# A graph layer on one core: the prologue put in a hand-set order, with x in pieces of 5 to 15 nodes a partition, the dst and edge-weight rows asked for later, and the check tables spread over the first passes

## The chip, the cores and the metric

The kernel runs on one core of one Trainium2 chip. The metric is the device time of an execution in microseconds (us). Three runs of the kernel before gave 2122.5, 2125.32 and 2127.98 us; the median is 2125.32.

Five engines work beside each other, each through its own list of instructions in order: TensorE (PE, matrix products), VectorE (DVE), ScalarE (ACT), GpSimd (POOL) and SyncE (SP). They wait for each other through semaphores. A DMA can be asked for from SP's, ACT's or POOL's list; an instruction that asks for a DMA may itself have to wait, and then everything behind it in that engine's list waits too.

## The reference

One layer of a graph network over N = 12500 nodes of D = 128 features and M = 200000 edges, sorted by target node `dst`:

```python
h = jnp.maximum(_layernorm(x, axis=-1), 0.0)
Qv = h @ W_Q.T;  Ku = h @ W_K.T
score = jnp.einsum('md,md->m', Qv[dst], Ku[src]) / np.sqrt(128) * jnp.exp(-edge_weight)
# of each target's edges the 16 with the highest scores are kept; softmax over them gives alpha
agg = segment_sum(alpha[:, None] * (h[src] @ W_msg.T), dst)
out = x + relu(h @ W_self.T + agg)
```

So every edge needs the normalised row h[src] of its source node, and these rows lie anywhere in the table.

## The kernel before

**Main loop (from L383).** Edges are cut into 112 windows of 14 chunks of 128 edges. For each chunk POOL issues one gather (L399, an indirect DMA): it fetches the 128 rows h[src] from the table `h_tab` in device memory into the tile `hs` (7 buffers of one window each). That makes 1563 gathers. A pass of the loop works on several windows at once: in pass i it lets go the gathers of window i+2 (`let_go`, L405: DVE copies the indices to `ix`, POOL gathers), computes scores of window i (L500), picks the 16 best of window i-2, forms weights of window i-3 and sums (L580, L590), and stores window i-5. The order of all this is written out by hand (`manual_schedule`), pass by pass. The gathers of windows 0 and 1 take their indices straight from `idx_all`, before the first pass. SP's list holds the loads of node rows (`load_nodes`, L422), of dst broadcast over the partitions (`load_dst`, L432) and the stores.

**Prologue (L103 to L356).** Before the loop, the kernel

- loads x in ten pieces of 10 nodes per partition on 125 partitions, each as two DMAs on SP (112 and 13 partitions, L235);
- normalises each piece: DVE computes mean and variance per node (L241, L242), ACT the square root (L245), DVE the reciprocal and the bias (L246, L248); DVE then applies them to two nodes of ten and ACT to eight (L252, L255); two SP stores write the piece to `h_tab` (L261);
- loads src, dst and edge weights as rows (121 partitions), four weight matrices and the window bounds `b_i`, all asked for on ACT;
- turns src, positions, decays and dst from rows to columns through PE (`to_columns`, L206): `idx_all`, `pos_all`, `dec_all`, `dst_all`;
- computes from dst the position of each edge among its target's edges (is_equal and a scan, L320, L321), window tables (`bb`, `nb`, `dlw`), and tables that check the assumptions of the fast path (`own`, `bad`, L322 to L356). If a check fails, a general path after the loop (`tc.If` on `any_i`) computes the layer instead; with these inputs it does not run.

The prologue's order on each engine is not written by hand: the framework's scheduler sets it. The memory of the pieces (`prep`) and of the late tables (`late`) is given back before the loop's tiles are made. Gathers read all of `h_tab`, so the first gather waits for the last store to it.

The transfers of SP and ACT take eight completion semaphores in turn; one that takes a semaphore again waits first for the transfer that had it last.

Of the kernel before, what the change touches and what calls it, by code (L numbers as in the profile page):

```python
# [20 lines left out]
P = 128  # L21
# [53 lines left out]
def gnn_layer(  # L75
# [58 lines left out]
    make_identity(nc, ident)  # L134
    ones = const.tile([P, 1], F32, name="ones")
    nc.vector.memset(ones, 1.0)
    onerow = const.tile([1, P], F32, name="onerow")
    nc.vector.memset(onerow, 1.0)
    zrow = const.tile([1, WW], BF16, name="zrow")
    nc.vector.memset(zrow, 0.0)  # L140
# [4 lines left out]
    for i in range(2):  # L145
        nc.gpsimd.memset(alz[i], 0.0)
        nc.gpsimd.memset(sl1[i][:, :, KM:], 1.0)
    slots = const.tile([P, KM], F32, name="slots")
    nc.gpsimd.iota(slots, pattern=[[1, KM]], base=0, channel_multiplier=0,
                   allow_small_or_imprecise_dtypes=True)  # L150
    nvec = const.tile([P, 1], F32, name="nvec")
    nc.gpsimd.iota(nvec, pattern=[[0, 1]], base=0, channel_multiplier=1,
                   allow_small_or_imprecise_dtypes=True)
# [15 lines left out]

    rows_pool = ctx.enter_context(tc.tile_pool(name="rows", bufs=1))  # L170


    with tc.tile_pool(name="edges", bufs=1) as ep:
        src_r = ep.tile([RR, RW], I32, name="src_r")
        dst_r = ep.tile([RR, HALO + RW], I32, name="dst_r")
        ew_r = ep.tile([RR, RW], F32, name="ew_r")

# [5 lines left out]

        nc.gpsimd.memset(src_r, 0)
        load_rows(src_r, src)
        nc.gpsimd.iota(dst_r, pattern=[[1, HALO + RW]], base=1 << 21, channel_multiplier=0)
        nc.gpsimd.memset(dst_r[0:1, 0:HALO], -1)
        nc.scalar.dma_start(dst_r[0:1, HALO:], dst[0:RW].rearrange("(p c) -> p c", p=1))
        if RF > 1:
            nc.scalar.dma_start(dst_r[1:RF, :], bass.AP(dst.tensor, dst.offset + RW - HALO,  # L190
                                                        [[RW, RF - 1], [1, HALO + RW]]))
        if REM:
            nc.scalar.dma_start(dst_r[RF:RF + 1, 0:HALO + REM],
                                dst[RF * RW - HALO:M].rearrange("(p c) -> p c", p=1))
        b_i = ep.tile([1, G], I32, name="b_i")
        nc.scalar.dma_start(b_i[:, 1:G], bass.AP(dst.tensor, dst.offset + EG - 1, [[EG, 1], [EG, G - 1]]))
        nc.gpsimd.memset(ew_r, 0.0)
        load_rows(ew_r, ew)

        wq_sb = ep.tile([P, P], F32, name="wq_sb")  # L200
        wk_sb = ep.tile([P, P], F32, name="wk_sb")
        ws_sb = ep.tile([P, P], F32, name="ws_sb")
        wm_sb = ep.tile([P, P], F32, name="wm_sb")
        for t, w in ((wq_sb, w_q), (wk_sb, w_k), (ws_sb, w_self), (wm_sb, w_msg)):
            nc.scalar.dma_start(t, w)
# [12 lines left out]
        src_f = src_r.bitcast(F32)  # L218
        nc.vector.tensor_copy(src_f, src_r)
        to_columns(src_f, 0, lambda at, p: nc.vector.tensor_copy(at(idx_all), p))  # L220

        HP = largest_divisor(N, P)
        HT = N // HP
        HG = largest_divisor(HT, 10)
        cuts = [(0, HP - HP % 16), (HP - HP % 16, HP)]
        by_part = lambda a: a[0:N, :].rearrange("(p t) d -> p t d", t=HT)
        with tc.tile_pool(name="prep", bufs=2) as prep:
            xs = []  # L230
            for g0 in range(0, HT, HG):
                xg = prep.tile([HP, HG, D], F32, bufs=HT // HG, name="xg")
                for a, b in cuts:
                    if a < b:
                        nc.sync.dma_start(xg[a:b], by_part(x)[a:b, g0:g0 + HG, :])  # L235
                xs.append(xg)
            for i, xg in enumerate(xs):
                mv = prep.tile([HP, HG, 2], F32, name="mv")
                for t in range(HG):
                    st = prep.tile([HP, 6], F32, bufs=4, name="st")  # L240
                    nc.vector.bn_stats(st, xg[:, t, :])  # L241
                    nc.vector.bn_aggr(mv[:, t, :], st)  # L242
                rs = prep.tile([HP, HG], F32, name="rs")
                nc.vector.tensor_scalar(rs, mv[:, :, 1], EPS, None, op0=OP.add)
                nc.scalar.sqrt(rs, rs)  # L245
                nc.vector.reciprocal(rs, rs)  # L246
                nm = prep.tile([HP, HG], F32, name="nmr")
                nc.vector.scalar_tensor_tensor(nm, mv[:, :, 0], -1.0, rs, op0=OP.mult, op1=OP.mult)  # L248
                few = HG // 5
                for t in range(HG):  # L250
                    if t < few:
                        nc.vector.tensor_scalar(xg[:, t, :], xg[:, t, :], rs[:, t:t + 1], nm[:, t:t + 1],  # L252
                                                op0=OP.mult, op1=OP.add)
                    else:
                        nc.scalar.activation(xg[:, t, :], xg[:, t, :], AF.Relu, bias=nm[:, t:t + 1],  # L255
                                             scale=rs[:, t:t + 1])
                if few:
                    nc.vector.tensor_scalar(xg[:, 0:few, :], xg[:, 0:few, :], 0.0, None, op0=OP.max)
                for a, b in cuts:
                    if a < b:  # L260
                        nc.sync.dma_start(by_part(h_tab)[a:b, i * HG:(i + 1) * HG, :], xg[a:b])  # L261
        zpad = ep.tile([P, D], F32, name="zpad")
        nc.gpsimd.memset(zpad, 0.0)
        nc.sync.dma_start(h_tab[N:N + P, :], zpad)
        nc.sync.dma_start(x_end[XT:XT + P, :], zpad)
        nc.sync.dma_start(x_end[0:XT, :], x[N - XT:N, :])

        pw = bank("s", 1)
        nc.tensor.matmul(pw[:, 0:P], lhsT=wq_sb, rhs=wk_sb, start=True, stop=True)
        nc.scalar.mul(a_qk, pw[:, 0:P], 1.0 / math.sqrt(D))  # L270
        pw = bank("s", 1)
        nc.tensor.transpose(pw[:, 0:P], ws_sb, ident)
        nc.tensor.transpose(pw[:, P:2 * P], wm_sb, ident)
        nc.scalar.copy(wselfT, pw[:, 0:P])
        nc.scalar.copy(wmsgT, pw[:, P:2 * P])


        row = ep.tile([1, 4, G + 1], F32, name="row")
        first, used, count = row[:, 0, 0:G], row[:, 1, 0:G], row[:, 2, 0:G]
        bad = ep.tile([P, 4], F32, name="bad")  # L280
        nc.vector.memset(bad, 0.0)
        nc.vector.memset(row, 0.0)
        nc.vector.tensor_scalar(row[:, 0, 1:G], b_i[:, 1:G], 1.0, None, op0=OP.add)
        nc.vector.memset(row[:, 0, G:G + 1], float(N))
        nc.vector.tensor_sub(count, row[:, 0, 1:G + 1], first)
        nc.vector.tensor_copy(used, first)
# [4 lines left out]
        nc.vector.memset(row_i[:, 1, :], 0)  # L291
        nc.vector.tensor_copy(row_i[:, 1, G - TAIL:G], row[:, 3, 0:TAIL])

# [6 lines left out]
        pb = bank("s", 1)  # L300
        nc.tensor.matmul(pb[:, 0:G], lhsT=onerow, rhs=used, start=True, stop=True)
        nc.tensor.matmul(pb[:, G:2 * G], lhsT=onerow, rhs=count, start=True, stop=True)
        bb = ep.tile([P, 2, G], F32, name="bb")
        nc.vector.tensor_copy(bb, pb[:, 0:2 * G].rearrange("p (a g) -> p a g", a=2))
        nc.vector.tensor_scalar(nb, bb[:, 0, :], nvec, -1.0, op0=OP.add, op1=OP.mult)
# [8 lines left out]
        RL = HALO + RW  # L314
        dst_f = dst_r.bitcast(F32)
        nc.vector.tensor_copy(dst_f, dst_r)
        h0 = ep.tile([RR, RL], F32, name="h0")
        h1 = ep.tile([RR, RL], F32, name="h1")
        nc.vector.memset(h0[:, 0:1], 0.0)
        nc.vector.tensor_tensor(h0[:, 1:RL], dst_f[:, 1:RL], dst_f[:, 0:RL - 1], op=OP.is_equal)  # L320
        nc.vector.tensor_tensor_scan(h1, h0, h0, 0.0, op0=OP.mult, op1=OP.add)  # L321
        nc.vector.tensor_reduce(bad[0:RR, 0:1], h1[:, HALO:RL], axis=AX.X, op=OP.max)  # L322
        nc.vector.tensor_scalar(bad[0:RR, 0:1], bad[0:RR, 0:1], float(KM), None, op0=OP.is_ge)
        nc.vector.scalar_tensor_tensor(h0[:, HALO:RL], dst_f[:, HALO - 1:RL - 1], 0.0, dst_f[:, HALO:RL],
                                       op0=OP.add, op1=OP.is_gt, accum_out=bad[0:RR, 1:2])
        nc.vector.memset(pos_all[:, RR * CPR:CW], 0.0)
        nc.vector.memset(dec_all[:, RR * CPR:CW], 0.0)
        to_columns(h1, HALO, lambda at, p: nc.vector.tensor_copy(at(pos_all), p))
        to_columns(ew_r, 0, lambda at, p: nc.scalar.activation(at(dec_all), p, AF.Exp, scale=-1.0))
        dst_all = ep.tile([P, CW], F32, name="dst_all")  # L330
        nc.vector.memset(dst_all[:, RR * CPR:CW], float(1 << 21))
        to_columns(dst_f, HALO, lambda at, p: nc.scalar.copy(at(dst_all), p))

        with tc.tile_pool(name="late", bufs=1) as lp:

            w0 = lp.tile([P, NJ], F32, name="w0")
            for j in range(NJ):
                nc.vector.memset(w0[:, j:j + 1], float(lead(j)))
            own = lp.tile([P, G, NJ], F32, name="own")
# [518 lines left out]
```

## Time and profile before

| what | us |
|---|---|
| median of three runs | 2125.32 |
| profiled execution: its own time / span in the trace | 2125.5 / 2123.7 |
| busy: PE, DVE, ACT, POOL | 1312.0, 1488.2, 626.7, 1544.1 |
| one gather: median, mean | 0.944, 0.975 |
| start of the first gather, start of the last | 79.86, 2084.51 |
| first copy of indices (`ix`) by DVE for a gather | 100.09 |
| issue of the first x load, of the last store of a piece | 0.78, 75.32 |

The span is counted from the first instruction of the program to the last; the profiled execution's own time is 1.8 us longer. A row of the timeline gives the start, the length, the engine and line, what is written and read, the shapes, how many instructions were merged, and in brackets the idle time of that engine before it and what ended it. "issue" there means that nothing that the profile shows was waited for. SPq and ACTq rows are DMA requests in an engine's list. In a view by stretches the last two numbers are the mean busy share of the core's 16 DMA engines and the GB/s they moved.

### The profile page before, as it was taken

To read this page: it belongs to the slowest core of one execution; us is meant where nothing else is said; L and a number is where in the kernel's file an instruction comes from. 1 tells how busy PE (TensorE), PEld (TensorE's weight loads), DVE (VectorE), ACT (ScalarE), POOL (GpSimd) and SP (SyncE) were. 2 spreads that over 40 slices of the span, in tenths; PEclk is the share of its full clock that TensorE was granted. 3 is DMA by queue.
4 is the path that set the end of the run, shared out by engine and by line. 5 is a ranking of instruction groups with operands and counts; after the bars stand their busy time and mean duration, and the time that the engine had idled before them with its cause. 6 is when DMAs were issued, how large, how long until landed. Compare 5 with 4: busy or idle time off the path is not lost. (4 is left out here: it accounts for less than half of the span.)

```text
span 2123.7 us, 43559 instructions
## 1 busy us (share of the span) xinstructions
PE 1312.0 (62%) x14574; PEld 1210.1 (57%) x14575; DVE 1488.2 (70%) x7474; ACT 626.7 (30%) x1225; POOL 1544.1 (73%) x1585
## 2 busy tenths in 40 slices
PE   1166666666666666666666666666666666666665
PEld 1155566555555655555555656565666666565654
DVE  7667677777776777767777767677777776777764
ACT  3442222222222222222222222222222222222220
POOL 1477777777777777777777777777777777777773
PEclk9977877877777877877777777777777787877787
DMA  8453343333343343333333334334433343333420
GB/s 220 146 162 116 119 120 119 120 119 119 120 119 119 116 122 115 115 112 119 118 119 119 119 119 120 119 119 120 120 119 120 119 120 120 119 119 119 120 67 24
DMA packets 118805, 253.18 MB, mean 119 GB/s; under 512 B 33030, under 2 KB 76297, under 8 KB 118558
## 3 DMA queue, kind: packets, MB, share of 16 engines
q1 hardware_dynamic: 67336, 144.92, 19.7%
q0 software_dynamic: 50144, 102.74, 19.1%
q10 hardware_dynamic: 1094, 2.69, 0.5%
q8 instruction: 115, 1.88, 0.4%
q14 instruction: 116, 0.95, 0.1%
HBM read 236.40 MB, written 14.40 MB: 118 GB/s over the span
## 5 line engine op out<-in xcount | busy, mean ns | idle before, releaser
L399 POOL DMA_INDIRECT hs<-h_tab,ix x1535 | 1495.9, 975 | 467.8 <-issue 335.9
L500 DVE SCALAR_TENSOR_TENSOR prod<-hs,dec_all,q 128x128 f32<-128x128 f32 x1674 | 516.9, 345 | 334.3 <-DMA hs<-h_tab,ix 319.1
L490 PE MATMUL q<-q,to_e 128*128 128x128 bf16 x5022 | 464.2, 254 | 33.1 <-DVE prod L500 32.3
L598 PE MATMUL s<-ident,agn 128*128 128x128 f32 x112 | 49.3, 440 | 662.2 <-DVE kept L579 661.7
L490 PEld LDWEIGHTS <-to_e 128*128 128x128 bf16 x5022 | 410.1, 116 | 56.0 <-issue 39.8
L590 PE MATMUL a<-hs,alz 128*128 128x128 f32 x3348 | 425.8, 281 | 0.8 <-DVE alz L580 0.8
L598 PEld LDWEIGHTS s<-ident,agn 128*128 128x128 f32 x112 | 20.2, 180 | 678.4 <-issue 676.7
L590 PEld LDWEIGHTS a<-hs,alz 128*128 128x128 f32 x3348 | 404.4, 197 | 1.2 <-DVE alz L580 1.1
L515 PE MATMUL e<-ow,sl 128*41 128x40 f32 x3348 | 251.3, 265 | 8.4 <-DVE sl L508 8.4
L515 PEld LDWEIGHTS e<-ow,sl 128*41 128x41 f32 x3348 | 235.7, 184 | 23.6 <-DVE sl L508 9.2
L466 ACT ACTIVATE far<-dstb,nb 128x1920 bf16<-128x1920 int32 x112 | 212.9, 1901 | 5.1 <-DMA dstb<-in_dst_dram 5.1
L471 ACT ACTIVATE to_e<-far 128x1920 bf16<-128x1920 bf16 x112 | 201.2, 1796 | 0.1
L602 ACT COPY aggT<-s 128x128 f32<-128x128 f32 x112 | 29.8, 266 | 507.8 <-PE s L598 507.8
L529 DVE TENSOR_SCALAR ell<-slots,e 128x40 f32<-128x40 f32 x112 | 28.3, 253 | 205.3 <-PE e L515 192.6
L546 ACT ACTIVATE e<-v,km 128x16 f32<-128x16 f32 x112 | 34.4, 308 | 363.5 <-DVE km L538 363.5
L500 DVE DVE_READ_ACCUMULATOR prod<-hs,dec_all,q 128x1 f32 x1674 | 139.1, 83 | 0.2
L414 DVE COPY ix<-idx_all 128x2 int32<-128x2 int32 (+1 forms) x768 | 132.7, 173 | 0.0
L575 ACT ACTIVATE up<-up 128x15 f32<-128x15 f32 x112 | 24.1, 215 | 336.5 <-DVE up L567 336.4
L595 ACT ACTIVATE agn<-a,rden 128x128 f32<-128x128 f32 x112 | 41.2, 368 | 209.8 <-PE a L590 209.8
L508 DVE TENSOR_TENSOR sl<-po,s 128x600 f32<-128x600 f32 x112 | 87.5, 781 | 3.9
L580 DVE TENSOR_TENSOR alz<-ow,kept 128x600 f32<-128x600 f32 x112 | 87.5, 781 | 3.8
L399 POOL DMA_INDIRECT hs<-h_tab,idx_all x28 | 33.7, 1203 | 77.6 <-DMA x_end<-zpad 69.4
(150 smaller groups left out, 1562.7 us busy)
## 6 DMA issues: line engine op xcount, KB each, us to landing
dstb<-in_dst_dram SPq DMA_DIRECT2D x111, 960.0 KB
hs<-h_tab,ix POOLq DMA_INDIRECT x1535
h_r<-h_tab SPq DMA_DIRECT2D x112, 64.0 KB
x_t<-in_x_dram SPq DMA_DIRECT2D x108, 64.0 KB
out_dram<-o SPq DMA_DIRECT2D x108, 64.0 KB
xg<-in_x_dram SPq DMA_DIRECT2D x10, 560.0 KB
h_tab<-xg SPq DMA_DIRECT2D x10, 560.0 KB
dst_r<-in_dst_dram ACTq DMA_DIRECT2D x1, 803.2 KB
```

What stands on the lines that cost most here:

```text
L399: nc.gpsimd.indirect_dma_start(out=T[g]["hs"][:, j, :], out_offset=None, in_=h_tab[0:N, :], in_offset=bass.IndirectOffsetOnAxis(ap=index(j ...
L414: nc.vector.tensor_copy(ix[:, j0:j1], idx_all[:, GC * g + j0:GC * g + j1])
L466: nc.scalar.activation(T[g]["far"][:, 0:n], T[g]["dstb"][:, 0:n], AF.Square, bias=nb[:, g:g + 1])
L471: nc.scalar.activation(T[g]["to_e"][:, 0:n], T[g]["far"][:, 0:n], AF.Relu, bias=1.0, scale=-1.0)
L490: nc.tensor.matmul(pq[:, (j - j0) * P:(j - j0 + 1) * P], lhsT=T[g]["to_e"][:, j * P:(j + 1) * P], rhs=upper(T[g]["q"][:, k, :]), start=(k ...
L500: nc.vector.scalar_tensor_tensor(prod, rows_of(g, j), dec_all[:, c:c + 1], T[g]["pq", b][:, (j % 4) * P:(j % 4 + 1) * P], op0=OP.mult, op1 ...
L508: nc.vector.tensor_tensor(sl1[g % 2][:, 0:n, 0:KM], T[g]["po"][:, 0:n, :], bc(T[g]["s"][:, 0:n], KM), op=OP.mult)
L515: nc.tensor.matmul(et[0:KM + 1, STEP * j:STEP * j + WN], lhsT=sl1[g % 2][:, j, :], rhs=T[g]["ow"][:, j, :], start=False, stop=(j == n - 1))
L580: nc.vector.tensor_tensor(alz[g % 2].rearrange("e (j w) -> e j w", w=WW + STEP)[:, 0:n, 0:WN], T[g]["ow"][:, 0:n, :], bc(kept[:, 0:n], WN) ...
L590: nc.tensor.matmul(T[g]["pa"][:, 0:P], lhsT=alz[g % 2][:, WW * j + PRE:WW * j + PRE + P], rhs=rows_of(g, j), start=(j == 0), stop=(j == n ...
L595: nc.scalar.activation(T[g]["agn"], T[g]["pa"][:, 0:P], AF.Copy, scale=T[g]["rden"])
L598: nc.tensor.transpose(so[:, 2 * P:3 * P], T[g]["agn"], ident)
```

## The change

1. **The prologue's order is set by hand**, engine by engine, under the same `manual_schedule` as the loop.
2. **x comes in eight pieces** of 5, 10, 15, 15, 15, 15, 15 and 10 nodes per partition. The statistics of a piece's first three nodes are put ahead of the normalising of the piece before it, the others behind.
3. **src is asked for first**, after a memset of its tile on DVE; then the weights and `b_i`. dst, the edge weights, the zero rows of `h_tab` and the copy `x_end` are asked for **on ACT, after piece 2**; the zero rows and `x_end` were on SP before. The four products with weights, the bounds and all dst tables come after the last piece.
4. **Check tables leave the prologue**: nine steps (`later`) are done by DVE one a pass, at the end of passes 1 to 9.
5. **Memory**: `hs` has 6 buffers instead of 7, `far` 1 instead of 2; `h_r`, `x_t` and `dstb` move to a pool that exists from the start.

```diff
-        HG = largest_divisor(HT, 10)
+    sizes = []
+    while sum(sizes) < HT:
+        left = HT - sum(sizes)
+        sizes.append(min(left, 5 if not sizes else 10 if len(sizes) == 1 or left <= 20 else 15))
...
+        nc.vector.memset(src_r, 0)
+        load_rows(src_r, src)
+        xs, t = [], 0
+        for i, n in enumerate(sizes):
+            xg = prep.tile([HP, n, D], F32, bufs=1, name=f"xg{i}")
+            for a, b in cuts:
+                nc.sync.dma_start(xg[a:b], by_part(x)[a:b, t:t + n, :])
...
+        for t, w in zip(ws, (w_q, w_k, w_self, w_msg)):
+            nc.scalar.dma_start(t, w)
+        nc.scalar.dma_start(b_i[:, 1:G], bass.AP(dst.tensor, dst.offset + EG - 1, [[EG, 1], [EG, G - 1]]))
...
+        stats(0, 0, sizes[0])
+        for i in range(len(xs)):
+            part = 0
+            if i + 1 < len(xs):
+                part = min(3, sizes[i + 1])
+                stats(i + 1, 0, part)
+            norm(i)
+            if i == 0:
+                nc.vector.tensor_copy(src_f, src_r)
+            if i == 1:
+                to_columns(src_f, 0, lambda at, p: nc.vector.tensor_copy(at(idx_all), p))
+            if i == 2:
+
+                nc.scalar.dma_start(dst_r[0:1, HALO:], dst[0:RW].rearrange("(p c) -> p c", p=1))
+                if RF > 1:
+                    nc.scalar.dma_start(dst_r[1:RF, :], bass.AP(dst.tensor, dst.offset + RW - HALO,
+                                                                [[RW, RF - 1], [1, HALO + RW]]))
+                if REM:
+                    nc.scalar.dma_start(dst_r[RF:RF + 1, 0:HALO + REM],
+                                        dst[RF * RW - HALO:M].rearrange("(p c) -> p c", p=1))
+                load_rows(ew_r, ew)
+                nc.scalar.dma_start(h_tab[N:N + P, :], zpad)
+                nc.scalar.dma_start(x_end[XT:XT + P, :], zpad)
+                nc.scalar.dma_start(x_end[0:XT, :], x[N - XT:N, :])
...
+            if part and part < sizes[i + 1]:
+                stats(i + 1, part, sizes[i + 1])
...
+        stage.close()
+        lp = stage.enter_context(tc.tile_pool(name="late", bufs=1))
...
+    later += [
+        far_from_start,
+        lambda: nc.vector.tensor_tensor(own_n[0], dl[0], bc(bb[:, 1, :], NJ), op=OP.is_lt),
+        lambda: nc.vector.scalar_tensor_tensor(own_n[0], dl[0], 0.0, own_n[0], op0=OP.is_ge, op1=OP.mult),
+        lambda: nc.vector.tensor_scalar(dl[0], dlw, -mid, None, op0=OP.add),
+        lambda: nc.vector.tensor_tensor(dl[0], dl[0], dl[0], op=OP.mult),
+        lambda: nc.vector.scalar_tensor_tensor(own_n[0], dl[0], (mid + 0.25) ** 2, own_n[0], op0=OP.is_gt,
+                                               op1=OP.mult, accum_out=badc[:, 2:3]),
+        lambda: nc.vector.tensor_reduce(badc[:, 0:1], pos_all, axis=AX.X, op=OP.max),
+        lambda: nc.vector.tensor_scalar(badc[:, 0:1], badc[:, 0:1], float(KM), None, op0=OP.is_ge),
+        all_checked,
+    ]
...
-                T[g]["hs"] = rows_pool.tile([P, GC, D], F32, name="hs", bufs=7)
+                T[g]["hs"] = rows_pool.tile([P, GC, D], F32, name="hs", bufs=6)
...
+            if i > 0 and later:
+                later.pop(0)()
```

`stats` takes bn_stats and bn_aggr of the named nodes and, after a piece's last node, adds EPS (DVE) and takes the root (ACT). `norm` takes the reciprocal and the bias on DVE, applies them to a fifth of the nodes on DVE and to the rest on ACT, and asks for the piece's two stores on SP.

## The prediction

> **What bounds the kernel now.** I read the page first (engine rows, gather row), then the timeline around the first and last gather, then what SP's queue waits for in the prologue, then short stretches with the DMA's share. Page, row by slice and costliest groups:
>
> ```profile
> POOL 1477777777777777777777777777777777777773
> ...
> L399 POOL DMA_INDIRECT hs<-h_tab,ix x1535 | 1495.9, 975 | 467.8 <-issue 335.9
> ```
>
> Timeline, rows of several stretches in order (start, length, engine, line, in brackets the idle time before it):
>
> ```profile
> 79.86 1.12 POOL L399 DMA_INDIRECT hs<-h_tab,idx_all  x1 [69.41 <-DMA x_end<-zpad]
> 81.28 0.97 POOL L399 DMA_INDIRECT hs<-h_tab,idx_all  x1 [0.30 <-issue]
> 82.14 1.79 DVE L342 TENSOR_TENSOR dl<-dst_all,bb 128x1568 f32<-128x1568 f32 x1 [2.50 <-ACT dst_all L332]
> 82.55 2.19 POOL L399 DMA_INDIRECT hs<-h_tab,idx_all  x1 [0.30 <-issue]
> ...
> 97.33 0.94 POOL L399 DMA_INDIRECT hs<-h_tab,idx_all  x1 [0.30 <-issue]
> ...
> 122.08 0.94 POOL L399 DMA_INDIRECT hs<-h_tab,ix  x1 [0.30 <-issue]
> ...
> 2084.51 0.97 POOL L399 DMA_INDIRECT hs<-h_tab,ix  x1 [0.30 <-DVE km L538]
> ```
>
> The 70% busy of POOL is a full engine: between any two of the 1563 gathers lie the same 0.30 us, so it never waits after 79.86 us. A plain gather is 0.944 us (median of the line) + 0.30 = 1.248 us. The stream lasts 2085.5 - 79.9 = 2005.6 us; 1563 x 1.248 = 1951; 55 us are gathers made longer. What follows the last gather (38.2 us) is the draining of six passes, which the change leaves alone. So span = first gather + stream + 38.2, and only two things can move the time: **when the first gather starts**, and **how much DVE lengthens gathers**. It starts when the last store to h_tab has landed (stores issued 74.96 and 75.32; 75.32 to 79.86 is 4.54 us).
>
> What holds the prologue: waits of SP's queue up to 80 us, ACT's idle, and the pace of normalising:
>
> ```profile
> SPq L235 <- DMA dst_r<-in_dst_dram: 9.3, 1, 9.3
> SPq L235 <- DMA src_r<-in_src_dram: 7.9, 1, 7.9
> ...
> 33.53 1.06 DVE L316 CAST dst_r<-dst_r 121x1728 f32<-121x1728 int32 x1 [4.79 <-DMA dst_r<-in_dst_dram]
> 36.95 3.18 ACT L255 ACTIVATE xg<-xg,nmr,rs 125x128 f32<-125x128 f32 x8 [11.99 <-DVE nmr L248]
> ...
> 57.27 3.18 ACT L255 ACTIVATE xg<-xg,nmr,rs 125x128 f32<-125x128 f32 x8 [0.55 <-DVE nmr L248]
> 61.11 3.19 ACT L255 ACTIVATE xg<-xg,nmr,rs 125x128 f32<-125x128 f32 x8 [0.55 <-DVE nmr L248]
> ```
>
> x loads queue behind dst and src: transfers of SP and ACT take eight completion semaphores in turn, and each waits for the last user of its own. DVE sat in the dst cast until 33.5, ACT idled 12 us, and nine of ten pieces were normalised after 36.9 at 3.83 us each.
>
> **The change part by part.**
>
> *Start.* src is now asked for after a memset on DVE (1.47 us on POOL's row; taken alike), at 2.5. Before, it was asked for at 14.52 and landed at 23.61 (dst's tail, which waits for that semaphore, is issued then): 9.1 us, beside x loads as now. So 11.6. In the built program the fourth weight's load waits for src's semaphore, and **ACT's first sqrt is queued behind it**: + weight 0.45, b_i 1.35, table load 1.28, sqrt 0.2 = 14.9; first activation 0.55 later.
>
> *Pieces 0 to 2.* From the first sqrt DVE sets the pace: a node's statistics take 0.26 us (rows of L241/L242 in the timeline). 0.4 for reciprocal and bias, 0.5 for its own nodes, src cast 1.03, 7 nodes 1.82, then 3 of the next 0.78, 0.4, 0.85, the four idx_all copies 2.88, 12 nodes 3.12, 0.2, 3 nodes 0.78, 0.4: piece 2's activations begin at 28.2, and its 12 (0.398 each) end at 33.0.
>
> *dst, weights of edges and tables, asked for after piece 2, on ACT's queue.* Eight issues stand in front of ACT's sqrt of piece 3. Seven find their semaphore free; x_end's zero pad waits until the 119-row dst load has landed. Queued behind: every later activation, so DVE (which has done piece 3's statistics and three nodes of piece 4) stops too, and the stores behind it. How long? Stretches of 2 us (PE, PEld, DVE, ACT, POOL, clock, DMA share, GB/s):
>
> ```profile
> 30.00:32.00 2.00, 0.00 (x0) 0.00 (x0) 0.00 (x0) 0.00 (x0) 0.00 (x0) 1.00 0.83 193
> 32.00:34.00 2.00, 0.00 (x0) 0.00 (x0) 0.47 (x1) 0.00 (x0) 0.00 (x0) 1.00 0.43 138
> ```
>
> With the dst load alone the DMA was 43% busy: seven of sixteen engines, 138 GB/s. The Trainium skill (DMA: Bandwidth & Descriptors, "Why a DMA increments its semaphore by 16 and not by 1") says that such a load uses the largest number up to 16 that divides its rows: 119 = 7 x 17. A fair share of the 250 GB/s of full stretches would give 0.82 MB / 250 = 3.3 us; by row and rule 0.82 / 138 = 6.0. I take 6.0, plus 2 for start and landing (an estimate: the first x data moved 1.4 us after its issue): issued by 33.5, landed at 41.5; the 16-engine value would put all that follows 2.7 us earlier. x_end's issues 0.46 + 0.68: ACT is free at 42.6, activations of piece 3 at 43.4. ACT's hold is some 9.6 us.
>
> *Pieces 3 to 7.* Ten nodes took 3.83 us with DVE full: 2.6 statistics, 1.23 rest. Fifteen: 3.9 + 1.23 + 0.42 (one node more on DVE, longer max) = 5.55; ACT needs 12 x 0.398 + 0.75 = 5.5, so neither hides the other. 4 x 5.55 = 22.2: 65.6; eight activations 3.2: 68.8; second store issued 69.25; + 4.54: **first gather at 73.8, 6.1 us earlier**. Stores of pieces 0 to 6 are hidden: they wait for dst and ew (about 47), but are 5.5 us apart and stores reach 300 GB/s (0.96 MB in 3.2).
>
> *Work after the first gather.* The is_equal and scan tables reuse piece memory and now wait for the stores, like the gather. To the first ix copy: 1.96 + 3.75 + pos_all copies behind PE 4.5 + dl 2.1 + w0 0.5 + dlw 1.9 + order test 1.9 + small ones 1.5 + places 1.6 = 20 us. Gathers 0 to 27 need none and last 28 x 1.248 = 35: covered by 15 us (before: 122.08 against a copy at 100.09).
>
> *DVE lengthens gathers.* 79.86 to 97.33 held nine gathers: 17.47 - 11.23 = 6.2 us lost, under 12.6 us of DVE tensor_tensor work: 0.47 us per us. ow and po, 1.56 us on end once a pass, cost 0.4; a single 0.78 us operation costs nothing. After the change, under the first gathers: is_equal 1.96 (0.5 to 0.9), dl, dlw, order test 5.9 (2.3 to 2.8), scan 3.75. For the scan no row: 0 to 1.8, I take 0.9. The nine later steps: six of 1.9 or 1.03 us, each beside sl and alz (0.78 each): between 0.5 alone and 1.4 in a block of 3.6: 3.3 to 7.8, take 5.8. The pos_all maximum is a tensor_reduce: the skill (SBUF — State Buffer, "Who interferes with whom") says these never contend, but that one instruction with two SBUF inputs does. Rows agree on reduce (gathers over L571 are not longer) and only half on the other: sl and alz have two SBUF inputs and alone cost 0; by the rule each step would block for its full 1.9, 11 us in all. The row decides. Sum 6 to 13, taken 9.8, less 6.2: **+3.6** (-0.2 to +7).
>
> *At no price.* hs with six buffers: in the trace the gather that would reuse a buffer six windows later starts 37 us or more after its sums were done; cover gone, it would cost up to a pass (18 us). far with one buffer: ACT writes and reads it in order. Node and dst loads from 74 on: SP only, passes have 15 us of cover.
>
> *Sum.* Against the profiled execution (span 2123.7, its own time 2125.5, median of the runs 2125.3): -6.1 + 3.6 = -2.5: 2123.0, or 2122.8 on the median.
>
> **The rivals.** 0.3% (6.4 us) is about what this measurement can tell from no change.
>
> *No hold* (faster): dst lands as soon as x does, ACT goes on at 33.7, DVE alone paces. First gather by the chain at 64; the bytes set a floor: 20 x (225 + 199 + 224 + 161) GB/s = 16.2 MB up to 80 us, 65 us at 250 GB/s. 66: -13.9 + 3.6 = 2115. For it: x loads should be over by 33. Against: the seven engines, and that the wait is in the program. Faster counts from a first gather at 69.9.
>
> *The dst load is as slow as before* (slower): at 15.63 it was asked for, at 33.36 its semaphore let an x load go, 17.7 us. Late x loads or ew beside it would do that: landed at 51.2, first gather 83.5, + 3.6 + 3.6 = 2132.5. It decides from a landing at 50.4. Against: half of the 17.7 was spent behind src.
>
> *The change doesn't do what it says* (same): the normalising moves forward, but the hold and the lengthened gathers give all of it back. This is the forecast's neighbour; at the high ends (contention +7, landing 2 us later) 2128.
>
> **How the numbers follow.** Forecast and its neighbour 0.65, 2117 to 2131; no hold 0.22 (2110 to 2119); slow dst 0.13 (2131 to 2136). Range 2114 to 2132: it leaves about 0.1 out at each end. Faster 0.22, same 0.65, slower 0.13.
>
> **What would show it.** First sqrt near 15; ACT idle some 9 us before the sqrt of piece 3, released by dst; activation blocks of 12 5.5 us apart; first gather 70 to 78; no POOL wait over 0.3 us after it; stream 2005.6 + 3.6; last gather to end 38. Wrong if ACT is free before 38 or after 50, if gathers wait for ix or hs, or if the pass steps lengthen no gather.

## The result and the profile after

The changed kernel takes **2127.2 us** (median of 20 executions, 2122.9 to 2131.4), the kernel before on the same chip 2121.9 us (20 executions, 2118.6 to 2128.0). The ratio is **1.0020 (95% interval 1.0013 to 1.0028)**: the change costs 2.8 to 5.9 us (the medians differ by 5.3) where a gain of 2.5 us was forecast. The time itself lies in the forecast range.

Page of the changed kernel: the POOL row by slice, and the group of gathers.

```profile
POOL 1377777777777777777777777777777777777773
...
L441 POOL DMA_INDIRECT hs<-h_tab,ix x1535 | 1492.8, 972 | 467.8 <-issue 337.4
```

POOL is the full engine as before. No gap between two gathers is longer than 0.32 us, so gathers wait neither for `ix` nor for one of the six `hs` buffers. Timeline of the changed kernel, several stretches in order (start, length, engine, line, idle time before it in brackets):

```profile
16.70 0.21 ACT L249 ACTIVATE rs<-rs 125x5 f32<-125x5 f32 x1
...
33.62 0.49 ACT L263 ACTIVATE xg<-xg,nm,rs 125x128 f32<-125x128 f32 x1 [1.33 <-DVE nm L256]
...
34.02 0.29 ACTq L286 DMA_DIRECT2D dst_r<-in_dst_dram  x1
...
45.62 0.37 ACTq L293 DMA_DIRECT2D x_end<-zpad  x1
46.71 0.21 ACT L249 ACTIVATE rs<-rs 125x15 f32<-125x15 f32 x1 [8.37 <-issue]
47.45 4.72 ACT L263 ACTIVATE xg<-xg,nm,rs 125x128 f32<-125x128 f32 x12 [0.53 <-DVE nm L256]
...
57.23 0.26 DVE L244 BATCH_NORM_STATS2 st<-xg 125x6 f32<-125x128 f32 x1
57.53 0.18 DVE L245 BATCH_NORM_AGGREGATE mv<-st 125x2 f32<-125x6 f32 x1
57.63 0.26 DVE L244 BATCH_NORM_STATS2 st<-xg 125x6 f32<-125x128 f32 x1
...
84.11 2.16 POOL L441 DMA_INDIRECT hs<-h_tab,idx_all  x1 [76.52 <-DVE h L332]
85.31 3.76 DVE L334 TENSOR_TENSOR_SCAN h<-h 121x1728 f32<-121x1728 f32 x1
86.57 3.27 POOL L441 DMA_INDIRECT hs<-h_tab,idx_all  x1 [0.30 <-issue]
...
2085.62 0.94 POOL L441 DMA_INDIRECT hs<-h_tab,ix  x1 [0.30 <-DVE km L581]
```

The first gather starts at 84.11 us, 4.25 us *later* than before (79.86); the forecast had 73.8. ScalarE (ACT) idled 8.4 us before 46.71, as forecast; but the activations of pieces 3 to 7 begin at 47.45, 55.25, 63.05, 70.86 and 76.17 us: **7.8 us apart, not 5.55**, up to piece 6; only piece 7, of ten nodes, follows after 5.3. VectorE (DVE) shows why: each aggregate starts only when its own statistics are done, 0.30 us after their start, and the next statistics follow it: one node per 0.40 us. In the kernel before, whose timeline follows, the scheduler had put the next node's statistics between the two, and they overlap:

```profile
58.94 0.27 DVE L241 BATCH_NORM_STATS2 st<-xg 125x6 f32<-125x128 f32 x1
59.12 0.17 DVE L242 BATCH_NORM_AGGREGATE mv<-st 125x2 f32<-125x6 f32 x1
59.20 0.27 DVE L241 BATCH_NORM_STATS2 st<-xg 125x6 f32<-125x128 f32 x1
```

Here a node takes 0.26 us. The aggregate at 59.12 starts before the statistics of 58.94 have ended (59.21), so it belongs to an earlier node; the names alone don't show that.

The spans of the two profiled executions differ by only 1.2 us (2123.7 and 2125.0). First gather: +4.25. Lengthening of gathers over the plain 0.944 us, in windows 0 to 8 (14 gathers each): 10.35 us before, 14.09 after, **+3.7**. In all later windows: 43.8 before, 36.8 after, -7.0. No other pair of traces of these two kernels showed such a fall (47.0 before and 49.7 after, 47.0 and 47.5 in the sets below), and two later runs that differ there only in the last three check steps are 6.0 us apart (45.9 in g1_both, 51.9 in g2_both_no_steps). I count it as spread between executions.

### The profile page after: what moved, and what is told of

It is laid out like the page before. It is cut to its first block, busy times and chain, and to the rows that moved or that the text cites. A ratio compares the mean times of both kernels' runs of the same rounds, so it can differ in the third digit from the quotient of the medians.

```text
span 2125.0 us, 43634 instructions
## 1 busy us (share of the span) xinstructions
PE 1313.5 (62%) x14574; PEld 1212.3 (57%) x14575; DVE 1502.3 (71%) x7470; ACT 624.9 (29%) x1222; POOL 1538.0 (72%) x1583
## 5 line engine op out<-in xcount | busy, mean ns | idle before, releaser
L441 POOL DMA_INDIRECT hs<-h_tab,idx_all x28 | 33.6, 1201 | 84.7 <-DVE h L332 76.5
```

Source lines behind the costliest of these rows:

```text
L441: nc.gpsimd.indirect_dma_start(out=T[g]["hs"][:, j, :], out_offset=None, in_=h_tab[0:N, :], in_offset=bass.IndirectOffsetOnAxis(ap=index(j ...
```

## The experiments

The kernels ran in five sets, each on one chip, each set timed against the kernel before on its own chip. The sets were not on the same chip: in the first and fourth the kernel before takes 2133 us and the gathers are the bound; in the second, third and fifth it takes 2797 to 2799 us and POOL waits (last section). There only the start of the first gather and the lengthening of single gathers can be read, and times say little. The changed kernel itself ran in sets 2, 3 and 4, not in set 1, and the kernel before has no trace in sets 1 and 4. Theories: A, the statistics pairs; B, the hold of ACT by the dst load; S, the nine check steps lengthen gathers; C, the longer streams of set 1 (from the first gather to the last: 2012 to 2020 us against 2002 to 2006 in the first pair) belong to the chip. For C speaks that the kernel before, too, takes 2133 us on that chip and 2122 on the first.

Readings of all runs, 5 (f1_after) to 22 executions each ("windows 2 to 8" is what those 98 gathers took over 0.944 us each; where the gathers are the bound the first step runs in window 2 and the seventh in window 8, elsewhere each runs a window later, so that the six large steps lie in windows 2 to 8 everywhere):

| run | first gather, us | windows 2 to 8, us | ratio to before (95%) | difference of medians, us |
|---|---|---|---|---|
| set 1, gathers bound: pairs apart (e1_paired) | 76.1 | 10.6 | 1.0019 (1.0013 to 1.0026) | +3.9 |
| requests on POOL (e2_on_pool) | 75.9 | 8.3 | 1.0028 (1.0019 to 1.0038) | +5.5 |
| no steps (e3_no_steps) | 82.8 | 2.9 | 1.0019 (1.0013 to 1.0026) | +4.3 |
| **both edits (e4_both)** | 66.4 | 6.3 | **0.9969 (0.9958 to 0.9980)** | -6.9 |
| set 2: before (e5_before) | 78.8 | 2.3 | 1.0008 (0.9991 to 1.0024) | +3.1 |
| after (e6_after) | 83.0 | 9.4 | 1.0011 (1.0001 to 1.0021) | +2.6 |
| both edits, steps in slices (e7_slices) | 66.7 | 3.8 | 0.9978 (0.9965 to 0.9991) | -6.9 |
| dst load cut (e8_split) | 78.8 | 8.7 | 0.9995 (0.9980 to 1.0010) | +0.6 |
| set 3: before (e9_before) | 79.9 | 2.6 | 0.9997 (0.9983 to 1.0011) | -1.2 |
| after (e10_after) | 84.8 | 8.9 | 1.0008 (0.9999 to 1.0017) | +1.7 |
| no steps (e11_no_steps) | 82.3 | 3.1 | 1.0010 (0.9996 to 1.0025) | +3.0 |
| both, slices (e12_slices) | 66.6 | 3.6 | 0.9987 (0.9974 to 0.9999) | -4.6 |
| set 4, gathers bound: after (f1_after) | 82.8 | 10.1 | 1.0043 (1.0030 to 1.0057) | +9.0 |
| no steps (f2_no_steps) | 84.0 | 3.3 | 1.0016 (1.0009 to 1.0022) | +4.0 |
| both, slices (f3_slices) | 68.4 | 4.1 | 0.9974 (0.9964 to 0.9985) | -5.7 |
| set 5: both (g1_both) | 67.8 | 8.5 | 0.9977 (0.9967 to 0.9987) | -7.6 |
| both, no steps (g2_both_no_steps) | 67.1 | 2.6 | 0.9976 (0.9964 to 0.9988) | -7.1 |
| both, steps at the end (g3_both_end) | 66.7 | 3.0 | 1.0003 (0.9988 to 1.0017) | -1.1 |

### A: pairs apart

```diff
 nc.vector.bn_stats(st, xg[:, t, :])
-nc.vector.bn_aggr(stat[i]["mv"][:, t, :], st)
+if held:
+    nc.vector.bn_aggr(stat[i]["mv"][:, held[0], :], held[1])
+held = (t, st)
...
+nc.vector.bn_aggr(stat[i]["mv"][:, held[0], :], held[1])
```

> The changed kernel with one edit: in the statistics of a piece, the bn_stats of the next node stands ahead of the bn_aggr of this one. Theory A (the hand-set order puts each bn_aggr straight behind the bn_stats that it needs, so that a node costs 0.40 us instead of 0.26, and DVE sets the pace of the prologue): a node falls to about 0.27, a piece of 15 from 7.8 us to about 5.6, the first gather from 84.1 to about 74, and the time by about 10 us, to some 2117. Rival B (the hold of ACT behind the dst load sets the first gather, the statistics are hidden beside it): the first gather moves by less than 4 us, to 80 or later.

Timeline of this kernel:

```profile
47.06 0.26 DVE L245 BATCH_NORM_STATS2 st<-xg 125x6 f32<-125x128 f32 x1
47.23 0.16 DVE L247 BATCH_NORM_AGGREGATE mv<-st 125x2 f32<-125x6 f32 x1
47.32 0.26 DVE L245 BATCH_NORM_STATS2 st<-xg 125x6 f32<-125x128 f32 x1
...
51.05 4.72 ACT L267 ACTIVATE xg<-xg,nm,rs 125x128 f32<-125x128 f32 x12 [0.99 <-DVE nm L260]
...
76.11 2.16 POOL L445 DMA_INDIRECT hs<-h_tab,idx_all  x1 [68.52 <-DVE h L336]
```

A node takes 0.26 us again (47.06 to 47.32), pieces follow each other 5.9 us apart (45.15, 51.05, 56.95), and the first gather is at 76.1, 6.7 to 8.7 us before that of the changed kernel in its four traces. A is shown for the first gather. The 10 us forecast for the time did not show: the ratio to the kernel before is 1.0019, that of the changed kernel 1.0020 in the first pair and 1.0043 in set 4, so the gain is between nothing and 5 us by the chip that it is compared with. Here the dst load took longer: requested at 29.28, and the request that waits for it went at 43.33, 14 us later. It was asked for 4.7 us earlier, with more of x still to load: in the trace 144 packets of x run while the dst load does, 35 in the changed kernel. That this is the cause was not tried.

### B: requests off ACT's list

The eight requests go to POOL's list, idle in the prologue, behind a one-column copy that makes them wait for piece 2; two memsets of POOL go ahead of them.

```diff
 if i == 2:
+    nc.gpsimd.tensor_copy(gate, stat[2]["rs"][:, 0:1])
-    nc.scalar.dma_start(dst_r[0:1, HALO:], dst[0:RW].rearrange("(p c) -> p c", p=1))
+    nc.gpsimd.dma_start(dst_r[0:1, HALO:], dst[0:RW].rearrange("(p c) -> p c", p=1))
...
```

> The changed kernel with one edit: the eight requests that stood on ACT after piece 2 (dst, edge weights, zero rows, x_end) stand on POOL, behind a one-column copy that waits for piece 2's square roots; ACT's list has none of them. Rival B (ACT held): the idle time of ACT before the square root of piece 3 goes, its activations start near 41.5 instead of 47.4 and the first gather comes at about 78, 6 us earlier; pieces stay 7.8 us apart. Theory A alone (statistics set the pace, the hold is hidden): first gather within 2 us of 84.1.

Timeline of this kernel:

```profile
31.38 0.19 POOL L287 COPY gate<-rs 125x1 f32<-125x1 f32 x1 [23.80 <-DVE rs L257]
31.52 0.74 POOL L288 DMA_DIRECT2D dst_r<-in_dst_dram  x1
31.56 4.72 ACT L266 ACTIVATE xg<-xg,nm,rs 125x128 f32<-125x128 f32 x12 [1.33 <-DVE nm L259]
...
39.36 4.72 ACT L266 ACTIVATE xg<-xg,nm,rs 125x128 f32<-125x128 f32 x12 [1.33 <-DVE nm L259]
...
75.94 2.08 POOL L442 DMA_INDIRECT hs<-h_tab,idx_all  x1 [39.90 <-issue]
```

From piece 2 to piece 3 it is 7.8 us, as between any later two: the hold is gone, and the first gather is at 75.9, about 7 to 9 us before that of the changed kernel. B is shown for the first gather. Both single edits start gathers some 3.5 us before the kernel before (its start is taken from other chips) and still take 4 to 5.5 us longer than it. A late first gather can't explain that; a longer stream, theory S, can.

### Both, and the steps alone

Without the nine steps the flags are set to zero; the checks of the input are left out in e3_no_steps, e11_no_steps, f2_no_steps and g2_both_no_steps, the layer itself is computed.

```diff
-    later += [
-        far_from_start,
...
-        all_checked,
-    ]
+    nc.vector.memset(any_i, 0)
+    nc.vector.memset(uns, 0.0)
```

> The changed kernel without the nine check steps of passes 1 to 9: that part of the check (window bounds of each edge, the largest position) is left out and the two flags are set to 0. Theory (each step of 1.9 us lengthens gathers beside it): the gathers of windows 3 to 8 are lengthened by about 2.3 us in all as in the kernel before, instead of 6.1; first gather unchanged at 84; time 3 to 4 us shorter. Rival (the steps lie in DVE's idle time and cost nothing; the lengthening comes from the passes' other work): windows 3 to 8 still 6 us.

> Both edits: statistics paired, and dst, edge weights, zero rows and x_end asked for on POOL. Theory A and B together: pieces 5.6 us apart from the first on, no hold, first gather at 66 to 68, the time 16 to 18 us below the changed kernel, about 2110, and 11 below the kernel before. Rival (the bytes bound it: 16 MB up to the first gather, stores at 300 GB/s behind the loads): first gather not before 72.

The two edits add up: 66.4 us for the first gather, 13 before the kernel before as other chips show it, and the time falls below it by 6.9 us (11 were expected). Leaving out the steps alone leaves the first gather late and lets windows 2 to 8 fall to 2.9 us.

### The dst load cut

```diff
-nc.scalar.dma_start(dst_r[1:RF, :], bass.AP(dst.tensor, dst.offset + RW - HALO,
-                                            [[RW, RF - 1], [1, HALO + RW]]))
+for r0, r1 in ((1, 113), (113, RF)):
+    nc.scalar.dma_start(dst_r[r0:r1, :], bass.AP(dst.tensor, dst.offset + r0 * RW - HALO,
+                                                 [[RW, r1 - r0], [1, HALO + RW]]))
```

The 119 rows become 112 and 7: one more request, so those behind it take other semaphores than before. The two unchanged kernels of this set stand beside it.

> The kernel before, unchanged, so that its trace and the others' come from one chip. All theories: time as the kernel before (ratio 1.000). First gather at 80 us (79 to 81). Theory S (the nine check steps lengthen gathers): windows 1 to 8, which have no step here, are lengthened by about 4 us together (0.4 to 0.6 each). Theory C (the longer streams of the runs so far belong to the chip, not to the kernels): the lengthening of the windows from 16 on is here within 0.03 us per window of that of the changed kernel in this set.

> The changed kernel, unchanged, on the same chip. First gather at 84 us (83 to 85), 4 us behind the kernel before. Theory S: windows 1 to 8 are lengthened by about 4 us more together than in the kernel before of this set, so the time is 4 + 4 = about 7 us longer (4 to 8; ratio 1.002 to 1.004). Rival (the later start alone is the loss): windows 1 to 8 as before, ratio 1.0018.

> The changed kernel with the dst load of 119 rows cut into 112 and 7 rows (nothing else). Theory of the seven engines (119 = 7 x 17 rows use seven DMA engines, 112 = 7 x 16 use sixteen): dst lands some 5 us earlier (landing 6 to 7 us after it was asked for instead of 11.3), ScalarE's hold ends 4 to 5 us earlier, first gather at 79 to 80 us instead of 84, time 4 to 5 us below the changed kernel. Rival (the load is slow because the loads of x are still under way beside it): landing and first gather within 1 us of the changed kernel's.

Timelines, first the changed kernel of this set:

```profile
33.55 0.29 ACTq L286 DMA_DIRECT2D dst_r<-in_dst_dram  x1
...
44.46 0.41 ACTq L293 DMA_DIRECT2D x_end<-zpad  x1
...
45.59 0.22 ACT L249 ACTIVATE rs<-rs 125x15 f32<-125x15 f32 x1 [7.69 <-issue]
...
83.00 2.16 POOL L441 DMA_INDIRECT hs<-h_tab,idx_all  x1 [75.40 <-DVE h L332]
```

and the one with the load cut:

```profile
34.76 0.33 ACTq L286 DMA_DIRECT2D dst_r<-in_dst_dram  x1
...
39.58 0.23 ACTq L190 DMA_DIRECT2D ew_r<-in_edge_weight_dram  x1
...
40.33 0.47 ACTq L293 DMA_DIRECT2D x_end<-zpad  x1
...
41.50 0.21 ACT L249 ACTIVATE rs<-rs 125x15 f32<-125x15 f32 x1 [2.42 <-DMA h_tab<-zpad]
...
78.77 2.14 POOL L441 DMA_INDIRECT hs<-h_tab,idx_all  x1 [71.18 <-DVE h L332]
```

From the request of the 119 rows to the request that waits for them (the zero pad) it was 10.9 us. For the 112 rows it was 4.8: here the second request for edge weights takes their semaphore and goes at 39.58, and the zero pad waits for another transfer. ACT's idle time falls from 7.7 to 2.4 us, and the first gather comes 4.2 us earlier. The packets in the two traces settle the cause. The 119 rows of 6912 bytes move from 34.47 to 43.61 us with seven at a time for most of it; cut, they move from 35.72 to 39.28, with sixteen or more at a time for half of it. The bytes are the same, so the rival (it is slow only because of x) falls: how the rows are cut decides. This agrees with the rule that the prediction took from the Trainium skill (DMA: Bandwidth & Descriptors, "Why a DMA increments its semaphore by 16 and not by 1": 119 rows go to seven engines); 112 rows divide by 16. It is a matter of the list, too: asked for from POOL's list in e2_on_pool, the same 119 rows move up to fifteen at a time and need 5.3 us (33.83 to 39.13).

For theory C this set adds that from window 16 on the two unchanged kernels' gathers are lengthened alike, 0.46 and 0.48 us a window.

### The price of the steps

> The kernel before, unchanged, once more: in the last set the gathers themselves were not the bound (POOL waited some 500 us for products of VectorE, at a granted clock of 0.73), so times could not be read. Where the gathers are the bound again (no wait of POOL over 0.32 us): first gather at 79 to 80 us, windows 1 to 8 lengthened by 2 to 4 us together, time as the kernel before.

> The changed kernel, unchanged. Theory (first gather + lengthened gathers): first gather at 83 to 84 us, 4.2 us behind the kernel before; windows 3 to 8 lengthened by 3.5 to 7 us more than its; sum +8 to +11 us, less what executions drift: ratio 1.002 to 1.005. Rival (first gather alone): +4 us, ratio 1.0018, and no difference to the run without check steps of this set.

> The changed kernel without the nine check steps (their flags are set to zero), as in the earlier run of this name, now beside the changed kernel. Theory: first gather as in the changed kernel (within 1.3 us), windows 3 to 8 as in the kernel before (2 to 3 us together), time 3.5 to 7 us below the changed kernel and 4 us above the kernel before. Rival: the same time as the changed kernel within 1.5 us.

> The changed kernel once more, for the price of the nine check steps where the gathers are the bound (no wait of POOL over 0.32 us after the first gather). Theory: first gather at 83 to 84 us, windows 3 to 8 lengthened by 6 to 9 us together; ratio 1.002 to 1.004. Rival (only the late first gather counts): the time of the run without steps within 1.5 us. If POOL waits again (time near 2800 us), only the first gather and the windows are read.

> The changed kernel without the nine check steps (flags zero). Theory: first gather within 1.3 us of the changed kernel's, windows 3 to 8 at 2 to 3 us together; time 3.5 to 6 us below the changed kernel. Rival: same time within 1.5 us.

Sets 2 and 3 give it by the trace: windows 2 to 8 take 2.3 and 2.6 us in the kernel before, 9.4 and 8.9 in the changed one, 3.1 without steps. Set 4 gives it by time too. POOL's gathers in windows 2 to 8 (stretch, its length, busy time of POOL and gathers, clock, DMA share, GB/s), first the changed kernel, then the one without steps:

```profile
124.77:257.28 132.51, 102.64 (x98) 0.72 0.33 104
```

```profile
126.28:251.93 125.65, 95.79 (x98) 0.74 0.34 108
```

The same 98 gathers take 6.9 us longer with the steps, and the medians differ by 4.9 us (its first gather is 1.2 us earlier). The changed kernel's gathers beside a step took up to 2.67 us. S is shown at 3 to 8 us (3.8 in the first pair of traces, 5.8 to 7.1 in sets 2 to 5, 3.4 to 7.7 in set 1 against e3_no_steps), and the rival, that only the late start counts, falls.

Why the first pair has 3.8 and set 4 has 6.9 can be read from single steps. A step and a reduce of set 4's changed kernel, then a step of the first pair's:

```profile
166.41 1.90 DVE L390 SCALAR_TENSOR_TENSOR own_n<-dl_n,own_n 128x1680 f32<-128x1680 f32 x1
166.47 2.66 POOL L441 DMA_INDIRECT hs<-h_tab,ix  x1 [0.30 <-issue]
...
243.09 1.79 DVE L395 TENSOR_REDUCE badc<-pos_all 128x1 f32<-128x1582 f32 x1
243.12 0.94 POOL L441 DMA_INDIRECT hs<-h_tab,ix  x1 [0.30 <-issue]
```

```profile
148.30 0.94 POOL L441 DMA_INDIRECT hs<-h_tab,ix  x1 [0.30 <-issue]
148.31 1.93 DVE L389 TENSOR_TENSOR own_n<-dl_n,bb 128x1680 f32<-128x1680 f32 x1
149.55 1.51 POOL L441 DMA_INDIRECT hs<-h_tab,ix  x1 [0.30 <-issue]
```

A gather that starts more than 0.03 us into a step with two inputs ends 0.82 us after the step does (169.13 and 168.31; 151.06 and 150.24). This holds within 0.01 us for all 45 such steps in the nine traces with whole steps. A gather that started just before the step (148.30) keeps its 0.94. So a step costs what is left of it when the next gather starts, less 0.13 us: 0.56 to 1.73 us. The one large step with a single input, 1.0 us long, cost 0.24 to 0.87. In the profiled execution of the first pair all five with two inputs met the gathers at the cheap moment, and the six large steps together cost 3.1 us; in set 4 three did not, and it was 6.5. The seventh step, the maximum of `pos_all`, is a reduce: beside it no gather in the nine traces is longer than a plain one, as the prediction had it.

### Keeping the steps without their price

The slices: six large steps cut into eight parts of 210 elements, one a pass over 48 passes.

```diff
+def slice_steps(k):
+    a, b = k * GS, min((k + 1) * GS, G)
...
-        far_from_start,
...
+    later += sum([slice_steps(k) for k in range(NS)], [])
```

> Statistics in pairs apart and the eight requests on POOL's list, as in the run with both, and the six large check steps each cut into eight slices of 14 windows (210 elements instead of 1680 a partition), one slice a pass over 48 passes. First gather at 66.4 us (65.5 to 67.5). Theory S with the row of single operations (a DVE operation of 0.78 us or less by itself lengthens no gather): windows 2 to 8 fall from 0.97 to about 0.5 us each, later ones stay; time 3 us below the run with both, 10 us below the kernel before (ratio 0.9953, 0.994 to 0.9965). Rival (the lengthening goes with the bytes, not with the length of one operation): the same 4 to 6 us spread over 48 windows, ratio 0.997 as with both edits.

> Statistics in pairs apart, the eight requests on POOL's list, check steps in slices of 14 windows over 48 passes. Theory: first gather at 66.5 us, 13 us before the kernel before; windows 3 to 8 within 1.5 us of the kernel before; sum -12, less up to 3 us for slices and drift: ratio 0.9935 to 0.9965. Rival (an earlier start is given back in the stream, as it half was in the last set): ratio 0.997 to 1.000.

> Pairs apart, requests on POOL's list, check steps in slices. Theory: first gather at 66.5 us; windows 3 to 8 within 2 us of the run without steps; time 16 us less (first gather) than the run without steps, 12 less than the kernel before: ratio 0.9935 to 0.9965. Rival: the stream gives half back, ratio 0.997 to 1.000.

In set 4 windows 2 to 8 fall to 4.1 us, but windows 9 to 50 take 25.6 us against 21.4 without steps: together 5.1 us over the run without steps, three quarters of the 6.9 us of whole steps. In set 3, where POOL waits, the same sum is 0.6 us. The ratio, 0.9974, is that of whole steps within its interval (0.9969, on another chip). My row "a single short operation costs nothing" did not carry over to a slice. The rival (the lengthening goes with the work, not with the length of one operation) fits no better: what decides is again whether a gather starts inside the slice. In set 4 one does so in 31 of the 48 slices and ends 0.81 to 0.82 us after the slice, 4.8 us in all; in the traces of sets 2 and 3 only two of 48 do, 0.2 us in all.

The steps behind the last gather:

```diff
-if i > 0 and later:
-    later.pop(0)()
+for _ in range(1 if i == G + 3 else len(later) if i == G + 4 else 0):
+    later.pop(0)()
```

> Pairs apart and the eight requests on POOL's list, check steps one a pass as in the changed kernel: the earlier run with both, again, as the base of this set. Where the gathers are the bound: first gather at 66.5 to 68.5 us, windows 3 to 8 at 5 to 8 us together, ratio to the kernel before 0.9965 to 0.9975.

> The same without the nine check steps (flags zero). Theory (steps cost 5 us wherever the first gather is): 4 to 6 us below the run with steps, windows 3 to 8 at 2.5 to 3.5 us together; ratio 0.9935 to 0.9955. Rival (the stream takes back what the prologue gives): within 1.5 us of the run with steps.

> The same with all nine check steps kept, but put behind the last gather: one into VectorE's idle time of 2.9 us before the last but one output, eight (about 11 us) after the last output tile. Theory: windows as without steps, 5 us gained; against it the end of the program waits for the flag, from nothing (the last 12 us of the span hide it) to 10 us (they don't). Taken: 3 us below the run with steps (from 5 below to 5 above).

Gathers are as free as without steps (3.0 us), but what follows the last gather grows from 64.0 us (g1) to 72.0. The flag is written here in the timeline:

```profile
2781.61 0.14 DVE L389 TENSOR_SCALAR any_i<-total 1x1 int32<-1x1 f32 x1
```

and the span ends at 2793.4, 11.7 us later: the end of the program waits for the flag, nothing hides it. The end grows by 8.0 us where windows 2 to 8 save 5.5, and the run without steps gains nothing over the run with them here, because in this set gathers are not the bound. No set with bound gathers ran g1 to g3. The best version found is both edits with the steps as they are: 0.9969 where gathers are the bound.

### The accounts

Where the gathers are the bound, first gather plus windows 2 to 8, against the mean of the kernel before's three traces (79.5 and 2.7 us), give the times within 3.5 us:

| run | first gather | windows 2 to 8 | sum | measured |
|---|---|---|---|---|
| e1_paired | -3.4 | +7.9 | +4.5 | +3.9 |
| e2_on_pool | -3.6 | +5.6 | +2.0 | +5.5 |
| e3_no_steps | +3.3 | +0.2 | +3.5 | +4.3 |
| e4_both | -13.1 | +3.6 | -9.5 | -6.9 |
| f1_after | +3.3 | +7.4 | +10.7 | +9.0 |
| f2_no_steps | +4.5 | +0.6 | +5.1 | +4.0 |
| f3_slices | -11.1 | +1.4, and +4.3 in windows 9 to 50 (against f2_no_steps) | -5.4 | -5.7 |

In e2's profiled execution the drain took 40.4 us instead of 38.3, which is 2.1 of its missing 3.5. The kernel before has no trace in these two sets; its numbers are from other chips, where its first gather was at 78.8 to 79.9 us.

## Why the prediction was wrong, step by step

*What bounds the kernel: right.* Span = first gather + stream + 38 us of drain; both terms named were the two that moved.

*Start: a little short.* The first square root ran at 16.7, not 14.9: src took 11.5 us (asked for at 2.67, the weight load that waits for it went at 14.15), not 9.1.

*Pieces 0 to 2: wrong by the pace.* Activations of piece 2 began at 33.6, not 28.2: 1.8 us from the start, and 25 nodes at 0.40 instead of 0.26 us (3.5 us). It cost the first gather little, since ACT's list sent the requests at 33.7 to 36, beside the activations of piece 2; I had them wait until these ended. (The prediction's terms add up to 28.1, not 28.2; this has no weight.)

*The hold: right in kind, short by 3.3 us.* I had 8 us from request to landing; it was 11.3 (34.02 to about 45.4). Stretches of 2 us of the changed kernel (PE, PEld, DVE, ACT, POOL, clock, DMA share, GB/s):

```profile
40.00:42.00 2.00, 0.00 (x0) 0.00 (x0) 0.95 (x6) 0.00 (x0) 0.00 (x0) 1.00 0.91 149
42.00:44.00 2.00, 0.00 (x0) 0.00 (x0) 0.00 (x0) 0.00 (x0) 0.00 (x0) 1.00 0.54 150
44.00:46.00 2.00, 0.00 (x0) 0.00 (x0) 0.00 (x0) 0.00 (x0) 0.00 (x0) 1.00 0.41 100
```

Until 42 other loads share the engines (0.91 busy); then they are about half busy (0.54 and 0.41), as the row of 32 to 34 us in the kernel before had shown. I gave it the speed that it has alone for all of its time: its packets took 9.7 us (34.97 to 44.71), not 6.0, beside 81 packets of edge weights and 35 of x. Seven engines: shown by the cut load and by the packets. Rival "no hold": the wait is there. Rival "slow dst load": it decides from a landing at 50.4, and it was 45.4; the slower result came by another way.

***Pieces 3 to 7*: this step failed.** It took 0.26 us a node from rows of the kernel before, where statistics and aggregates of different nodes alternate, and used it for an order in which the source puts each aggregate right behind its statistics. 15 x 0.14 = 2.1 us a piece; 28.7 us for the four steps from piece 3 to piece 7 (three of 7.8, one of 5.3) instead of 22.2. With pairs apart these four took 23.0. The sum of the error at the first gather: 4.05 up to piece 3's activations, 6.5 here, -0.3 behind: 10.3 us, from 73.8 to 84.1. With pairs apart and the hold left in, the forecast's 73.8 is missed by 2.3 us only: 76.1.

*DVE lengthens gathers: right in sum, and by luck in part.* +3.6 forecast, +3.7 in the first pair of traces. Window 0: I had 4.0 us of new lengthening there for the 6.2 that go away; it took 6.72 against 6.66, so nothing went away. The scan was the largest miss: beside it a gather took 3.27 us, 2.3 too long, against 0.9 taken (0 to 1.8). The steps: 5.8 forecast, 3.8 in that pair, 5.8 to 7.1 in sets 2 to 5. In the first pair the two misses, +2.3 in window 0 and -2.0 in the steps, cancel. The 11 us that the prediction set against its row, each step blocking for its full length, is too much in every trace. But the rule behind it, an exclusive lock (the Trainium skill, SBUF — State Buffer, "Who interferes with whom"), agrees with the single steps: the gather waits for the whole rest of the step, and only how much is left differs. The prediction's own rows had it: `dl` ends at 83.93 and the gather beside it at 84.74, 0.81 us later. That `sl` alone costs 0 was a matter of when it runs: the nine gathers of the kernel before that start well inside one are all lengthened. And 6.2 us under 12.6 us of work is 0.49 us per us, not 0.47.

*Hidden work: right.* Six `hs` buffers, one `far`, node loads and the first index copy (at 102.6, 18.5 us after the first gather; needed 35 after it) caused no gap over 0.32 us between gathers.

What stays open: in the first pair the two terms add up to 8 us and the medians differ by 5.3 (2.8 to 5.9). In set 4 the same kernels differ by 9.0 (6.4 to 12.2), against 10.7 by the terms. The steps' 3.1 us in one profiled execution and 6.5 in the other would make most of the difference between the two pairs, if other executions are like these; no trace shows that they are. What the later windows gave back in the first pair stays open.

## What to carry to other kernels

When an order is set by hand over a schedule that a planner made, look in the trace at what the planner had put between dependent instructions; a time per item read from an interleaved stream holds only while the interleaving does. A DMA request that waits for a semaphore holds everything behind it in its list, so it belongs in the list of an engine with nothing to do, and the rows of a load asked for from ACT's list should be a multiple of sixteen. Where one engine streams without a gap, count only its start and what makes its instructions longer; vector work moved under the stream of gathers is paid there, whole or in slices, by where it falls on them; the reduce was free.

## What the runs showed of the hardware that I had not expected

The same program took 2122 to 2133 us in the first pair and two sets, and 2797 to 2799 us in three others, on other chips. The costliest line of weighted sums in the kernel before, first in the profile of the beginning, then in e5_before (busy time, mean ns, idle time before it):

```profile
L590 PE MATMUL a<-hs,alz 128*128 128x128 f32 x3348 | 425.8, 281 | 0.8 <-DVE alz L580 0.8
```

```profile
L399 POOL DMA_INDIRECT hs<-h_tab,ix x1535 | 1498.3, 976 | 1107.4 <-issue 523.8 <-DVE prod L500 504.6 <-DVE kept L579 32.7
L590 PE MATMUL a<-hs,alz 128*128 128x128 f32 x3348 | 611.9, 346 | 125.2 <-issue 116.1 <-DMA hs<-h_tab,ix 7.3 <-DVE alz L580 0.8
```

The matrix products with 32-bit data take 346 ns instead of 281, at a mean granted clock of 0.726 instead of 0.795; a gather is as long as before (976 and 975 ns), but POOL is now idle for 1107 us before its gathers instead of 468, and 505 of them end with DVE's products. An earlier first gather is then worth about half: 12 to 13 us earlier gave 5 to 8. Why these chips are slower was not tried. Besides: a request in ACT's list goes out beside activations that stand before it and are still running (first request of the changed kernel at 33.72, activations of piece 2 from 33.62 to 38.34).
